# Convolution filter matrices on 112 partitions, first-stage stores on the scalar engine's queue, raw weights loaded in thirds

## Chip, cores and metric

The kernel runs on one core of a Trainium2 chip. The metric is the device time of the core in microseconds, median over runs; less is better. One execution was also recorded by the hardware profiler. Its engines are called PE (matrix multiply), PEld (weight load of PE), DVE (vector), ACT (scalar), POOL (GpSimd) and SP (which only issues transfers here).

## What is computed

The input `x` is 32 images of 384 channels of 28 by 28, all in float32. The reference is a ConvNeXt block followed by a gating layer:

```
y = depthwise_conv7x7(x, dw_w) + dw_b              # 384 channels, each with its own 7x7 filter
y = layernorm over channels(y) * ln_g + ln_b
y = gelu(y @ w1 + b1)                              # 384 -> 1536
y = grn(y) (per image, over the pixels) ; y = y @ w2 + b2        # 1536 -> 384
x = x + y
out = sigmoid(x + logits(mean, max, min of each channel of x))
```

## The kernel before

The work has a first stage (the depthwise convolution, with the preparation of the weights) and then, image by image, an up projection (`up`), a down projection (`down`) and the gate (`gate_store`). The two projections use schemes with fewer products than the plain matrix product: blocks of the weights are added and subtracted beforehand into combined weights (`form_w`, 15 for `w1`, 38 for `w2`), which the first stage stores to DRAM (`u1d`, `u2d`) and the later stages load again. Everything after the first stage keeps its instructions and nearly its order; the change is in the first stage and in the few operations that lead out of it.

**How the convolution is done on PE.** A row group of `RW`=4 image rows is one contraction. In the kernel before, each image row is padded from 28 to `PW`=32 columns, so a group is 128 elements on 128 partitions. For each channel a banded matrix of the 49 filter taps is needed. A sequence of `FL`=355 numbers for each channel lies in DRAM (`fs`), and row p of the matrix is that sequence read from p elements further on; `load_t` (L416) makes the matrices of `TC`=8 channels with one transfer, `tmat<-fs`, whose DRAM side steps by one element for each partition. A step `s` of the stage handles 8 channels for all 32 images; there are `NK`=48 steps and four buffers `tmat`. `load_t(s+3)` is issued at the start of step `s`.

**Input.** `load_x` (L449) loads tile `i`: 32 channels of 4 images, one (channel, image) pair on each of 128 partitions, 784 elements each. Eight tiles make a group of 32 channels, that is four steps. `pad_x` (L468) copies a tile to a padded buffer `xpad` (POOL for the first eight tiles, ACT for the other 88), `turn_x` (L477) transposes it in seven 128-column pieces on PE into PSUM (`pt`), and copies those with DVE and ACT to `xt`. `spread` spreads these over the steps of the group before.

**Convolution.** `conv` (L653) does a pair of channels: six matmuls into one PSUM tile `pc` of four; DVE transposes the pair in 32 by 32 blocks into `yt` (L682) and adds it to `acc` (L690), ACT squares it into `sq` (L696), POOL adds the squares to `ssum` (L702). After four pairs `yt` is stored to `yd` in DRAM (L837). Two buffers hold `yt`.

**Weights.** `w1` and later `w2` are loaded raw into `ws` (table `later`, issued at L789); each of these is preceded by a one-column copy on POOL that makes the load wait (L788). `center_w` folds the layer norm into `w1`. From step `U1`=11 on, `form_w` (L543) makes the combined `w1` blocks, from `U2`=23 on those of `w2`, on POOL (L550, L556) and ACT (L553), three buffers `u` in turn; the store of a block is issued at the end of the step after (L853).

**Order.** The Tile framework records the instructions of each engine and may move those that are not marked; `keep` marks an instruction to stay in program order. Within an engine, and within the list of transfers that an engine issues, order is fixed: in the kernel before SP issues all the loads and the stores `yd<-yt`, `u1d<-u`, `u2d<-u`. The lines that decide what follows a wait are

```
load_t(s + 3)
...
nc.sync.dma_start(yd[:, s * TC : (s + 1) * TC, :], yt)
...
for dst, u in stores:
    nc.sync.dma_start(dst, u)
```

**Way out of the stage.** The last two steps are done in halves of 16 images; `first_image` prepares image 0, `finish` (L710) turns `acc` and `ssum` into the factor of the layer norm and stores it (`rsd`), and `normed` (L307) applies it to image 1 with the reloaded `rb`.

Of the kernel before, what the change touches and what calls it, by code (L numbers as in the profile page):

```python
# [8 lines left out]
F32 = mybir.dt.float32  # L9
AF = mybir.ActivationFunctionType  # L10
ALU = mybir.AluOpType
AX = mybir.AxisListType

P = 128
C = 384
CB = C // P
FF = 4 * C
# [12 lines left out]
RW = 4  # L30
NJ = HW // RW
PW = P // RW
XC = 32
TC = 8
YC = 16
# [162 lines left out]
def convnext_gate_kernel(  # L198
# [109 lines left out]
    def normed(b, cbs=range(CB)):  # L308

        if b not in accs:  # L310
            accs[b] = (
                xp.tile([P, CB, NT], F32, tag="x", name=f"acc_{b}") if b == 1 else room_acc
            )
        for cb in cbs:
            nc.vector.scalar_tensor_tensor(  # L315
                accs[b][:, cb].rearrange("p (r w) -> p r w", w=HW), rows(yis[b][:, cb]),
                dwb_t[:, cb : cb + 1], rows(rbs[b]), ALU.add, ALU.mult,
            )

    def affine(eng, out, in_, mul, add):  # L320
        if eng is nc.vector:
# [38 lines left out]
    with ExitStack() as one:  # L360
        tp = one.enter_context(tc.tile_pool(name="tp", bufs=1))
        xtp = one.enter_context(tc.tile_pool(name="xtp", bufs=2))
        ufp = one.enter_context(tc.tile_pool(name="ufp", bufs=3))
        ycp = one.enter_context(tc.tile_pool(name="ycp", bufs=2))
        psx = one.enter_context(tc.tile_pool(name="psx", bufs=3, space=bass.MemoryType.PSUM))
        psb = one.enter_context(tc.tile_pool(name="psb", bufs=1, space=bass.MemoryType.PSUM))
        psc = one.enter_context(tc.tile_pool(name="psc", bufs=4, space=bass.MemoryType.PSUM))
        sqp = one.enter_context(tc.tile_pool(name="sqp", bufs=2))
        finp = one.enter_context(tc.tile_pool(name="finp", bufs=1))

        scr = yip.tile([P, CB, NQD, YR], F32, tag="yi", name="scr")
# [27 lines left out]


        NT2 = 4
        tmat = [tp.tile([P, TC, FL], F32, name=f"tmat_{i}") for i in range(NT2)]
        nc.vector.memset(tab, 0.0)

        def sequences(cb):
# [12 lines left out]
        def load_t(s, parts=1):  # L418
            base = fs[s * TC // P]
            n = TC // parts  # L420
            for i in range(parts):
                nc.sync.dma_start(
                    tmat[s % NT2][:, i * n : (i + 1) * n, :].rearrange("p c m -> p (c m)"),
                    bass.AP(
                        tensor=base.tensor,
                        offset=base.offset + (s * TC % P + i * n) * FL,
                        ap=[[1, P], [1, n * FL]],
                    ),
                )


        NPAD = 3
        xpad = [tp.tile([P, HW, PW], F32, name=f"xpad_{i}") for i in range(NPAD)]
        for t in xpad:
            nc.gpsimd.memset(t[:, :, HW:], 0.0)
        NX = C // XC
        NG = B // NB
        NXI = 8
# [26 lines left out]

        keep = tc.keep_in_program_order

        def pad_x(i):  # L468
            dst = xpad[i % NPAD][:, :, :HW]
            src = xis.pop(i).rearrange("p (r w) -> p r w", w=HW)  # L470
            if i < NG:
                nc.gpsimd.tensor_copy(dst, src)
            else:
                keep(nc.scalar.activation(dst, src, AF.Identity))

        def turn_x(i, h, xt, eng=nc.vector):

            g = i % NG
            xv = xt.rearrange("p c (j b) -> p j c b", j=NJ)
            j0, j1 = 4 * h, min(NJ, 4 * h + 4)  # L480
            pt = psx.tile([P, 4, P], F32, tag="pt", name=f"pt_{i}_{h}")
            for j in range(j0, j1):
                keep(
                    nc.tensor.transpose(  # L484
                        pt[:, j - j0, :],
                        xpad[i % NPAD][:, j * RW : (j + 1) * RW, :].rearrange("p r w -> p (r w)"),
                        ident,
                    )
                )
            dst = xv[:, j0:j1, :, g * NB : (g + 1) * NB]  # L490
            src = pt[:, : j1 - j0, :].rearrange("p j (c q) -> p j c q", q=NB)
            if eng is nc.vector:
                keep(eng.tensor_copy(dst, src))
            else:
                keep(eng.activation(dst, src, AF.Identity))  # L495

        def new_xt(k):
            return xtp.tile([P, XC, N], F32, tag="xt", name=f"xt_{k}")


        w1r = ws.rearrange("p (k f) -> p k f", f=FF)
        w1v = ws.rearrange("p (k t m c) -> p t k m c", t=KT, m=3, c=P)
        w2v = ws.rearrange("p (t k m c) -> p t k m c", t=KD, k=4, c=P)
        U1, U2 = 11, 23
        stores = []
        SG = 20

# [93 lines left out]

        AHEAD = NG

        def pad_next(i):
            if i < GT:
                pad_x(i)
                if i + AHEAD < GT:
                    load_x(i + AHEAD)

        for i in range(AHEAD):  # L610
            load_x(i)
        xt = new_xt(0)
        for i in range(NG):
            pad_x(i)
            if i == 0:
                load_t(0, 2)
                nc.sync.dma_start(dwb, cvec[0:1, :].broadcast_to([P, C]))
            if i == NG - 2:
                for cb in range(CB):
                    if cb:  # L620
                        keep(sequences(cb))
                    keep(nc.scalar.dma_start(fs[cb][P:, :], zrow))
            if i == NG - 2:

                nc.gpsimd.tensor_copy(tmat[1][:, 0, :1], xpad[i % NPAD][:, 0, :1])
                load_t(1)
            if i + AHEAD < GT:
                load_x(i + AHEAD)
            for h in range(2):
                turn_x(i, h, xt, (nc.vector, nc.scalar)[h])  # L630
        pad_next(NG)

        later = {
            2: (
                ws.rearrange("p (cb f) -> p cb f", f=FF),
                w1.rearrange("(cb p) f -> p cb f", p=P),
            ),
            U2 - 3: (
                ws.rearrange("p (fb c) -> p fb c", c=C),
                w2.rearrange("(fb p) c -> p fb c", p=P),  # L640
            ),
            1: (cv, cvec.rearrange("v (cb p) -> p v cb", p=P)),
            4: (fv, fvec.rearrange("v (fb p) -> p v fb", p=P)),
            6: (awt[:, 0], aw[0].rearrange("(cb p) r -> p cb r", p=P)),
            7: (awt[:, 1], aw[1].rearrange("(cb p) r -> p cb r", p=P)),
            8: (w22b, w22.broadcast_to([P, R])),
# [64 lines left out]
        def finish(half, b0, b1):  # L711

            def part(v):
                return v.rearrange("p (j b) -> p j b", b=B)[:, :, b0:b1]

            rs, s2 = (part(fin[:, i]) for i in range(2))
            mu, va = (part(acc[:, i]) for i in range(2))
            keep(nc.vector.tensor_tensor(mu, mu, va, ALU.add))
            keep(
                nc.vector.tensor_reduce(  # L720
                    s2,
                    ssum.rearrange("p c (j b) -> p j b c", b=B)[:, :, b0:b1],
                    AX.X, ALU.add,
                )
            )
            keep(nc.vector.tensor_scalar(mu, mu, dws, 1.0 / C, ALU.add, ALU.mult))
            keep(nc.vector.tensor_tensor(va, mu, mu, ALU.mult))
            keep(nc.vector.scalar_tensor_tensor(va, s2, 1.0 / C, va, ALU.mult, ALU.subtract))
            keep(nc.vector.tensor_scalar(va, va, 0.0, EPS, ALU.max, ALU.add))
            nc.scalar.activation(s2, va, AF.Sqrt)  # L730
            keep(nc.vector.reciprocal(rs, s2))
            keep(nc.vector.transpose(fin[:, 2], fin[:, 0]))
            nc.sync.dma_start(rsd[half], fin[:, 2])

        STEPS_K = SK * PAIRS
# [4 lines left out]
        def spread(k, q, xn):  # L740
            for n in plan[q]:
                g, h = divmod(n, 2)
                i = k * NG + g
                if h == 0:
                    pad_next(i + 1)
                turn_x(i, h, xn, (nc.vector, nc.scalar)[h])

        def first_image(part):

# [25 lines left out]
        for s in range(NK):  # L775
            k, si = divmod(s, SK)
            if s + 3 < NK:
                if s == 0:
                    for i in range(2, 4):
                        nc.gpsimd.tensor_copy(tmat[i][:, 0, :1], xpad[i % NPAD][:, 0, :1])  # L780
                        if i == 2:
                            load_t(i)
                load_t(s + 3)
# [44 lines left out]
            elif s < NK - 2:  # L828
                for c2 in range(PAIRS):
                    conv(s, c2, yt, xt, 0, B)  # L830
                    q = (s - U1 + 4) * PAIRS + c2
                    if 0 <= q < 4 * PAIRS:
                        for n in range(q * 3 // 2, (q + 1) * 3 // 2):
                            center_w(n)
                    if k + 1 < NX:
                        spread(k + 1, si * PAIRS + c2, xn)
                nc.sync.dma_start(yd[:, s * TC : (s + 1) * TC, :], yt)  # L837
                yt = new_yt(f"yt_{s + 1}")
                if s == 35:
                    yi = yis[0] = yip.tile([P, CB, NQD, YR], F32, tag="yi", name="yi_0")  # L840
# [9 lines left out]
                gate_weights()  # L850
                nc.vector.tensor_reduce(dws, dwb, AX.X, ALU.add)
            for dst, u in stores:
                nc.sync.dma_start(dst, u)  # L853
            stores.clear()
            for i in range(NS):
                if s != U1 + i * 3 // 5:
# [62 lines left out]
    def up(b, hooks):  # L919
# [6 lines left out]
        for t2 in range(0, KT, 2):  # L926
            for i, (opnd, _, bk, first, acts) in enumerate(UPSTEPS):
                for t in (t2, t2 + 1):
# [16 lines left out]
                    for src, how, to in acts:  # L945
                        p, d = banks[t, src][:, :NH], z[to]
                        if how == "copy":
                            ins = nc.scalar.activation(d, p, AF.Identity)  # L948
                            if b < 2:
                                tc.keep_in_program_order(ins)  # L950
                        elif how == "add":
                            nc.vector.tensor_tensor(d, d, p, ALU.add)  # L952
# [335 lines left out]
```

## Time and profile before

| | |
|---|---|
| time, median of 3 runs (lowest to highest) | 3091.12 us (3090.16 to 3092.08) |
| profiled execution: its own time, its span | 3089.71 us, 3087.7 us |
| PE busy | 3011.4 us (98%) |
| ACT, DVE, POOL busy | 1808.4, 1994.1, 2438.7 us |
| moved by DMA in the first 540 us | 173.12 MB, 321 GB/s |
| first convolution matmul, last convolution matmul | 20.2 us, 540.7 us |

The page has a row of digits for each engine over the span in 40 equal slices of 77 us (9 is 90% or more). In answers by stretch of time a row gives begin and end, length, then busy time and number of instructions for PE, PEld, DVE, ACT and POOL, the granted PE clock as a share of full speed, the busy share of the 16 DMA engines, and GB/s. In lists of waits a row gives who waited, for whom, the total in us, how often, and the longest. In lists of transfers a row gives the number, the size of each, and the median from issue to landing.

### The profile page before, as it was taken

What the parts mean: (1) busy time and instruction counts of PE and PEld (TensorE: products, weight loads), DVE (VectorE), ACT (ScalarE), POOL (GpSimd) and SP (SyncE); (2) the same over time, 40 slices, a digit from 0 to 9 for tenths busy, and PEclk for the clock granted to TensorE, in tenths of its full rate; (3) what the DMA queues carried; (4) which work ended last, traced back from release to release, by engine and by line L of the source; (5) the groups of instructions that cost most, each with busy time, mean ns of one, the idle gap of its engine ahead of it and who ended that gap; (6) DMA issues with size and microseconds to landing.
All of it is one profiled execution on the core that took longest, in us unless ns stands there. A gap on an engine that the chain in (4) does not pass through costs nothing.

```text
span 3087.7 us, 44113 instructions
## 1 busy us (share of the span) xinstructions
PE 3011.4 (98%) x14435; PEld 2434.4 (79%) x14435; DVE 1994.1 (65%) x4554; ACT 1808.4 (59%) x3004; POOL 2438.7 (79%) x1829
## 2 busy tenths in 40 slices
PE   7999989889999999999999999999999999999998
PEld 7999989467777777777777777777777777777777
DVE  4565546766666666666666666666666666666666
ACT  3454555556666666666666666666666666666661
POOL 3365857389888888888888888888888888888897
PEclk9999999999999999999999999999999999999999
DMA  9799988555666666666666666666666666666546
GB/s 367 263 333 356 335 324 264 174 165 188 202 199 196 200 198 200 198 197 200 199 199 200 199 200 202 200 203 200 202 201 202 199 200 201 201 201 202 194 153 201
DMA packets 288476, 673.24 MB, mean 218 GB/s; under 512 B 31199, under 2 KB 111610, under 8 KB 282234
## 3 DMA queue, kind: packets, MB, share of 16 engines
q1 hardware_dynamic: 275156, 631.62, 62.2%
q10 hardware_dynamic: 13094, 38.80, 3.3%
q8 instruction: 118, 1.93, 0.3%
q14 instruction: 108, 0.88, 0.1%
HBM read 575.57 MB, written 94.76 MB: 217 GB/s over the span
## 4 chain that ended last, share of the span: by engine, by line
PE 86%; DVE 5%; POOL 4%; DMA 2%; ACT 1%; issue 1%; SPq 0%; DVEq 0%; ACTq 0%; POOLq 0%
PE ph_C L941 14%; PE ph_A L941 12%; PE ph_B L941 11%; PE pz_A L1071 8%; PE pz_C L1071 8%; PE pz_F L1071 7%; PE pz_D L1071 7%; PE pc L675 4%; PE pc L679 3%; PE pc L677 3%; PE pz_H L1071 2%; PE pz_I L1071 2%; PE pz_E L1071 2%; PE pt L484 2%; DVE room L315 2%
## 5 line engine op out<-in xcount | busy, mean ns | idle before, releaser
L324 ACT ACTIVATE y<-y,fv,gsc 128x784 f32<-128x784 f32 x372 | 359.1, 1031 | 464.8 <-DVE gsc L979 464.8
L1032 POOL TENSOR_TENSOR d_room<-y 128x588 f32<-128x588 f32 x253 | 364.4, 1442 | 289.6 <-PE pz_B L1071 192.2
L941 PE MATMUL ph_C<-room,ws 128*128 128x392 f32 x1240 | 464.6, 497 | 9.1 <-DVE y L952 3.8
L900 ACT ACTIVATE y<-y,b1f 128x784 f32<-128x784 f32 x384 | 349.9, 944 | 200.9 <-DVE y L958 179.0
L941 PE MATMUL ph_B<-room,ws 128*128 128x392 f32 x1240 | 459.6, 493 | 6.8 <-ACT y L948 4.3
L941 PE MATMUL ph_A<-room,ws 128*128 128x392 f32 x1240 | 458.8, 492 | 2.0 <-POOL room L356 2.0
L1032 POOL TENSOR_TENSOR d_room<-d_room,y 128x588 f32<-128x588 f32 x308 | 440.7, 1435 | 16.8
L941 PEld LDWEIGHTS ph_C<-room,ws 128*128 128x128 f32 x1240 | 234.0, 191 | 193.8 <-DVE y L956 28.5
L941 PEld LDWEIGHTS ph_A<-room,ws 128*128 128x128 f32 x1240 | 235.8, 190 | 175.6 <-POOL room L356 2.7
L941 PEld LDWEIGHTS ph_B<-room,ws 128*128 128x128 f32 x1240 | 234.7, 190 | 171.2 <-ACT y L948 5.0
L702 POOL TENSOR_TENSOR ssum<-ssum,sq 128x896 f32<-128x896 f32 (+1 forms) x100 | 201.5, 2015 | 184.2 <-ACT sq L696 183.8
L913 ACT ACTIVATE junk<-y 128x784 f32<-128x784 f32 x384 | 329.0, 857 | 9.0
L1032 POOL TENSOR_TENSOR d_room<-y,d_room 128x588 f32<-128x588 f32 x214 | 306.0, 1436 | 26.9 <-PE pz_D L1071 15.8
L356 POOL TENSOR_TENSOR room<-room 128x392 f32<-128x392 f32 x303 | 303.4, 1018 | 11.9
L696 ACT ACTIVATE sq<-pc,dwb 128x224 f32<-128x224 f32 x368 | 144.5, 444 | 227.0 <-DVE acc L690 211.4
L1032 POOL TENSOR_TENSOR y<-y 128x588 f32<-128x588 f32 x180 | 258.6, 1437 | 7.1
L682 DVE STREAM_TRANSPOSE yt<-pc 128x448 f32<-128x448 f32 x184 | 119.5, 649 | 208.3 <-PE pc L679 194.9
L954 DVE TENSOR_TENSOR y<-y,ph_B 128x392 f32<-128x392 f32 x256 | 137.2, 556 | 155.2 <-ACT y L900 123.5
L952 DVE TENSOR_TENSOR y<-y,ph_C 128x392 f32<-128x392 f32 x384 | 212.4, 561 | 25.2
L675 PE MATMUL pc<-xt,tmat 128*128 128x224 f32 x736 | 203.2, 358 | 2.6 <-ACT xt L495 2.6
L1071 PE MATMUL pz_A<-d_room,u 128*128 128x196 f32 x1050 | 202.9, 329 | 0.1
L1071 PEld LDWEIGHTS pz_A<-d_room,u 128*128 128x128 f32 x1050 | 178.8, 190 | 7.7 <-POOL d_room L1032 0.4
(265 smaller groups left out, 6374.6 us busy)
## 6 DMA issues: line engine op xcount, KB each, us to landing
u<-u2d SPq DMA_DIRECT2D x487, 384.0 KB, 3.8
ws<-u1d SPq DMA_DIRECT2D x384, 320.0 KB, 3.0
tmat<-fs SPq DMA_DIRECT2D x47, 1420.0 KB, 8.8
ws<-u2d SPq DMA_DIRECT2D x121, 384.0 KB, 3.8
yi<-yd SPq DMA_DIRECT2D x95, 448.0 KB, 6.3
yd<-yt SPq DMA_DIRECT2D x46, 896.0 KB, 6.3
x<-in_x SPq DMA_DIRECT2D x32, 1176.0 KB, 5.5
out<-x ACTq DMA_DIRECT2D x31, 1176.0 KB, 9.2
```

Source lines behind the costliest of these rows:

```text
L324: eng.activation(out, in_, AF.Identity, bias=add, scale=mul)
L356: tc.keep_in_program_order(eng.tensor_tensor(d, o[in0], o[in1], op))
L675: keep(nc.tensor.matmul(po, t[:, c, P : 2 * P], xc, start=True, stop=False))
L696: nc.scalar.activation(part(sq)[:, cy % SQ + ci], part(pc[:, :, :N])[:, ci], AF.Square, bias=dwb[:, cc + ci : cc + ci + 1], scale=1.0,)
L702: nc.gpsimd.tensor_tensor(part(ssum), part(ssum), part(sq), ALU.add)
L900: ins = nc.scalar.activation(y, y, AF.Gelu, bias=b1f[:, f : f + 1], scale=1.0)
L913: ins = nc.scalar.activation(junk, ys[b][:, f, :], AF.Square, accum_out=ssqs[b][:, f : f + 1])
L941: nc.tensor.matmul(banks[t, bk][:, :NH], wts[t][:, i % UG, :], o[opnd], start=(first == 1), stop=True, skip_group_check=True,)
L952: nc.vector.tensor_tensor(d, d, p, ALU.add)
L954: nc.vector.tensor_tensor(d, d, p, ALU.subtract)
L1032: nc.gpsimd.tensor_tensor(d[0], o[a][0], o[c][0], ALU.add if sign == "+" else ALU.subtract)
L1071: nc.tensor.matmul(pz[:, :NQ4], wt[:, i % UD, t, :], o[opnd][0][:, t, :], start=(first and t == 0), stop=(t == KD - 1), skip_group_check=True,
```

## The change

The padded copy is gone, with `xpad` and its memsets: row groups are 4 times 28 = 112 elements (`KP`), a group is transposed as it was loaded, and the filter matrices and `xt` lie on 112 partitions. The DRAM side of `tmat<-fs` now counts 4 by 28 rows, so as to leave out the four padding rows in each 32. The stores of the first stage move from SP's queue to ACT's and are kept in program order. `w1` and `w2` are loaded in three parts each, at steps 3, 4, 5 and 21, 22, 23; `U1`, `U2` become 12 and 24; `ufp` has four buffers in place of three, `sqp` three in place of two. The next `x` tile of a slot is loaded after the transposes of the tile in it, not after its padding. The matrices of `center_w`'s second part come four at a time. `normed` of image 1 stays in program order, the nine DVE operations of `finish` lose their `keep` and may be moved, and so may the copies of image 0 in its first two blocks of `up`.

```
+KP = RW * HW
@@ normed
-            nc.vector.scalar_tensor_tensor(
+            ins = nc.vector.scalar_tensor_tensor(
...
+            if b == 1:
+                tc.keep_in_program_order(ins)
@@ pools
-        ufp = one.enter_context(tc.tile_pool(name="ufp", bufs=3))
+        ufp = one.enter_context(tc.tile_pool(name="ufp", bufs=4))
-        sqp = one.enter_context(tc.tile_pool(name="sqp", bufs=2))
+        sqp = one.enter_context(tc.tile_pool(name="sqp", bufs=3))
-        tmat = [tp.tile([P, TC, FL], F32, name=f"tmat_{i}") for i in range(NT2)]
+        tmat = [tp.tile([KP, TC, FL], F32, name=f"tmat_{i}") for i in range(NT2)]
@@ load_t
                         offset=base.offset + (s * TC % P + i * n) * FL,
-                        ap=[[1, P], [1, n * FL]],
+                        ap=[[PW, RW], [1, HW], [1, n * FL]],
@@ pad_x
-        def pad_x(i):
-            dst = xpad[i % NPAD][:, :, :HW]
-            src = xis.pop(i).rearrange("p (r w) -> p r w", w=HW)
-            if i < NG:
-                nc.gpsimd.tensor_copy(dst, src)
-            else:
-                keep(nc.scalar.activation(dst, src, AF.Identity))
@@ turn_x
-            pt = psx.tile([P, 4, P], F32, tag="pt", name=f"pt_{i}_{h}")
+            pt = psx.tile([P, 4, P], F32, tag="pt", name=f"pt_{i}_{h}")[:KP]
...
-                        pt[:, j - j0, :],
-                        xpad[i % NPAD][:, j * RW : (j + 1) * RW, :].rearrange("p r w -> p (r w)"),
-                        ident,
+                        pt[:, j - j0, :], xis[i][:, j * KP : (j + 1) * KP], ident
@@
-            return xtp.tile([P, XC, N], F32, tag="xt", name=f"xt_{k}")
+            return xtp.tile([KP, XC, N], F32, tag="xt", name=f"xt_{k}")
-        U1, U2 = 11, 23
+        U1, U2 = 12, 24
-        def pad_next(i):
-            if i < GT:
-                pad_x(i)
-                if i + AHEAD < GT:
-                    load_x(i + AHEAD)
+        def load_next(i):
+            del xis[i]
+            if i + AHEAD < GT:
+                load_x(i + AHEAD)
+        def hold(dst, i):
+            nc.gpsimd.tensor_copy(dst, xis[i][: dst.shape[0], :1])
@@ later
-            2: (
-                ws.rearrange("p (cb f) -> p cb f", f=FF),
-                w1.rearrange("(cb p) f -> p cb f", p=P),
-            ),
...
+                3 + cb: (
+                    ws.rearrange("p (cb f) -> p cb f", f=FF)[:, cb],
+                    w1[cb * P : (cb + 1) * P, :],
+                )
+                for cb in range(CB)
...
+                U2 - 3 + i: (
+                    ws.rearrange("p (fb c) -> p fb c", c=C)[:, 4 * i : 4 * i + 4],
+                    w2[4 * i * P : (4 * i + 4) * P, :].rearrange("(fb p) c -> p fb c", p=P),
+                )
+                for i in range(3)
@@ finish
-            keep(nc.vector.tensor_tensor(mu, mu, va, ALU.add))
+            (nc.vector.tensor_tensor(mu, mu, va, ALU.add))
...
@@ spread
-                if h == 0:
-                    pad_next(i + 1)
                 turn_x(i, h, xn, (nc.vector, nc.scalar)[h])
+                if h:
+                    load_next(i)
@@ center_w
-                    q = (s - U1 + 4) * PAIRS + c2
-                    if 0 <= q < 4 * PAIRS:
+                    q = (s - U1 + 5) * PAIRS + c2
+                    if 0 <= q < 2 * PAIRS:
                         for n in range(q * 3 // 2, (q + 1) * 3 // 2):
                             center_w(n)
+                    elif q in (2 * PAIRS + 2, 2 * PAIRS + 5, 2 * PAIRS + 8):
+                        n = FB + 4 * ((q - 2 * PAIRS) // 3)
+                        for i in range(4):
+                            center_w(n + i)
@@ stores
-                nc.sync.dma_start(yd[:, s * TC : (s + 1) * TC, :], yt)
+                keep(nc.scalar.dma_start(yd[:, s * TC : (s + 1) * TC, :], yt))
...
             for dst, u in stores:
-                nc.sync.dma_start(dst, u)
+                keep(nc.scalar.dma_start(dst, u))
@@ up
-                            if b < 2:
+                            if b == 1 or (b == 0 and t2):
```

More of the change, by code (lines that the diff above doesn't have):

```diff
@@ L426, in load_t @@
                         offset=base.offset + (s * TC % P + i * n) * FL,
-                        ap=[[1, P], [1, n * FL]],
+                        ap=[[PW, RW], [1, HW], [1, n * FL]],
                     ),
                 )
[L432 to L435, printed above, removed]
         NX = C // XC
@@ L466, in convnext_gate_kernel @@
         keep = tc.keep_in_program_order
-        def pad_x(i):
-            dst = xpad[i % NPAD][:, :, :HW]
-            src = xis.pop(i).rearrange("p (r w) -> p r w", w=HW)
-            if i < NG:
-                nc.gpsimd.tensor_copy(dst, src)
-            else:
-                keep(nc.scalar.activation(dst, src, AF.Identity))
+        keep = tc.keep_in_program_order
         def turn_x(i, h, xt, eng=nc.vector):
@@ L613, in convnext_gate_kernel @@
         for i in range(NG):
-            pad_x(i)
             if i == 0:
@@ L623, in convnext_gate_kernel @@
             if i == NG - 2:
-                nc.gpsimd.tensor_copy(tmat[1][:, 0, :1], xpad[i % NPAD][:, 0, :1])
+                hold(tmat[1][:, 0, :1], i)
                 load_t(1)
-            if i + AHEAD < GT:
-                load_x(i + AHEAD)
             for h in range(2):
                 turn_x(i, h, xt, (nc.vector, nc.scalar)[h])
-        pad_next(NG)
+            load_next(i)
         later = {
-            2: (
-                ws.rearrange("p (cb f) -> p cb f", f=FF),
-                w1.rearrange("(cb p) f -> p cb f", p=P),
-            ),
[L638 to L641, printed above, removed]
+            **{
+                3 + cb: (
[3 more added lines that the diff above has]
+                for cb in range(CB)
+            },
+            **{
+                U2 - 3 + i: (
[3 more added lines that the diff above has]
+                for i in range(3)
+            },
             1: (cv, cvec.rearrange("v (cb p) -> p v cb", p=P)),
-            4: (fv, fvec.rearrange("v (fb p) -> p v fb", p=P)),
+            2: (fv, fvec.rearrange("v (fb p) -> p v fb", p=P)),
             6: (awt[:, 0], aw[0].rearrange("(cb p) r -> p cb r", p=P)),
@@ L717, in finish @@
             mu, va = (part(acc[:, i]) for i in range(2))
-            keep(nc.vector.tensor_tensor(mu, mu, va, ALU.add))
-            keep(
+            (nc.vector.tensor_tensor(mu, mu, va, ALU.add))
+            (
                 nc.vector.tensor_reduce(
@@ L725, in finish @@
             )
[L726 to L729, printed above, removed]
+            (nc.vector.tensor_scalar(mu, mu, dws, 1.0 / C, ALU.add, ALU.mult))
+            (nc.vector.tensor_tensor(va, mu, mu, ALU.mult))
+            (nc.vector.scalar_tensor_tensor(va, s2, 1.0 / C, va, ALU.mult, ALU.subtract))
+            (nc.vector.tensor_scalar(va, va, 0.0, EPS, ALU.max, ALU.add))
             nc.scalar.activation(s2, va, AF.Sqrt)
-            keep(nc.vector.reciprocal(rs, s2))
-            keep(nc.vector.transpose(fin[:, 2], fin[:, 0]))
+            (nc.vector.reciprocal(rs, s2))
+            (nc.vector.transpose(fin[:, 2], fin[:, 0]))
             nc.sync.dma_start(rsd[half], fin[:, 2])
@@ L743, in spread @@
                 i = k * NG + g
-                if h == 0:
-                    pad_next(i + 1)
                 turn_x(i, h, xn, (nc.vector, nc.scalar)[h])
+                if h:
+                    load_next(i)
         def first_image(part):
@@ L779, in convnext_gate_kernel @@
                     for i in range(2, 4):
-                        nc.gpsimd.tensor_copy(tmat[i][:, 0, :1], xpad[i % NPAD][:, 0, :1])
+                        hold(tmat[i][:, 0, :1], NG)
                         if i == 2:
```

## The prediction

> **What bounds the kernel now.** I read the page's slices first, then the first stage in stretches, then PE's waits there, then the transfers.
>
> ```profile
> PE   7999989889999999999999999999999999999998
> ...
> DMA  9799988555666666666666666666666666666546
> ```
>
> PE is busy nearly everywhere. The first seven slices (to 540 us) differ from the rest in the last row: there the DMA engines too are nearly full. The change works there.
>
> ```profile
> 20.00:120.00 100.00, 93.18 (x586) 89.11 (x587) 51.28 (x89) 46.19 (x104) 34.65 (x23) 0.97 0.96 350
> 120.00:160.00 40.00, 36.20 (x232) 34.97 (x232) 23.75 (x44) 16.22 (x36) 14.35 (x10) 0.96 0.61 213
> 160.00:240.00 80.00, 79.76 (x503) 76.36 (x502) 47.37 (x82) 46.06 (x102) 50.25 (x32) 1.00 0.98 341
> 240.00:520.00 280.00, 263.89 (x1615) 252.37 (x1614) 152.20 (x265) 147.01 (x332) 185.52 (x130) 0.97 0.91 327
> ```
>
> Undisturbed (160 to 240 us) PE is full, and a step takes about 10.2 us. Two resources bound the stage together: PE, and right behind it the DMA engines, 0.91 to 0.98 busy. PE's pauses are short:
>
> ```profile
> PE pt L484 <- ACT xpad L474: 22.0, 5, 8.8
> PE pt L484 <- POOL xpad L472: 6.8, 2, 6.2
> PE ph_C L941 <- DVE y L952: 4.9, 3, 3.8
> PE ph_B L941 <- ACT y L948: 4.3, 1, 4.3
> PE pm L588 <- DVE ws L597: 3.8, 2, 3.1
> ```
>
> From 20.2 to 540.7 us they sum to 26.7. After a long pause matmuls take twice their time for a while: from 60 to 80 us 72 matmuls (11.2 us at the undisturbed pace) and a pause of 6.3 leave 2.5 us lost; over the five long pauses about 10. Behind the pauses: at 64 us a store `yd<-yt` landed after 16 us behind the whole `w1`; at 300 and 415 us ACT sat for a `u` buffer (7.3, 9.2 us); at 248 us DVE waited for POOL's copy at L788.
>
> ```profile
> q1 hardware_dynamic: 53640, 171.41, 88.8%
> ...
> tmat<-fs SPq DMA_DIRECT2D x47, 1420.0 KB, 8.8
> yd<-yt SPq DMA_DIRECT2D x46, 896.0 KB, 6.3
> room<-in_x SPq DMA_DIRECT2D x84, 392.0 KB, 6.6
> ```
>
> The filter matrices are 68 MB of the stage's 171: the largest transfer by far, spread over 16 engines.
>
> [...] loads with 128, 112 or 16 rows outermost show 16 completion events each; `scr<-in_wfcT` (24 rows, 130.4 us) shows 13[...]; the one-row stores `fs<-scr` show 2. `room<-in_x` counts 32 by 4 in DRAM and 128 in SBUF, and shows 16. No transfer of before has fewer than 12 engines and many bytes. [...] the trace has the halving (two matmuls of L675 that otherwise take 0.38 us take 0.75 from 72 to 77 us).
>
> **The change part by part.**
>
> (1) *The filter load.* Its SBUF side has 112 rows outermost, its DRAM side 4 (times 28, step 32 and 1). [...] So each of the 47 loads (and the first in two halves) runs on four engines, 28 rows on each, in place of 8 rows on each of 16. Bytes fall by 12.5%, bytes per loaded engine rise 3.5 times. Price, from the trace's packet records: a row of 11360 bytes is one packet, median 426 ns (26.7 GB/s; mean 489 over the stage, 435 from 120 to 160 us, where the engines are less full). The work of one of the four engines over the stage, by medians:
> filter rows 48 x 28 x 0.426 = 572.5 us; `x` tiles 96 x 8 x 0.124 = 95.2; `yd` 46 x 8 x 0.272 = 100.1; `u1d` 15 x 32 x 0.027 = 13.0; `u2d` 38 x 8 x 0.065 = 19.8; `w1`, `w2` 12; constants, `fs` and the first `u1d` reloads 11. Sum 823 us.
> By the means of 120 to 160 us it is 882, by those of the whole stage 940. Below the medians: packets overlap a little (the busy share goes to 1.03 from 60 to 80 us), up to 6%, 775. I take 840: near the medians, since with four engines full and twelve mostly idle the total is under 200 GB/s, and the long packets of before come when 350 are moved.
> That is 17 us per step against PE's 10.2, or 12.7 with the half clock after each pause: PE waits for every filter load, with `load_t(s+3)` always issued ahead, so the four engines never run dry. First load at 1.3 us; some 6 us of the 840 follow the last filter load; from its landing PE has two steps in halves less what can start before, 14 us (18.9 for all of it, of which step 46's first half, 4.7, needs only the load before). Last convolution matmul: 1.3 + 840 - 6 + 14 = 849, before 540.7: **+309**. Lookahead of four buffers hides latency, not a missing rate.
>
> (2) *Padding gone.* ACT loses 88 copies of 0.858 us (75.5), POOL 8 of 0.84. Both lie beside PE's wait for the filter: nothing. Without that cover it takes ACT out of the chain DVE, ACT, pad, transpose, where 22.0 + 6.8 us were lost.
>
> (3) *Stores on ACT's queue.* 46 + 53 transfers, 0.3 to 0.9 us each to issue by the rows of L815, so 30 to 90 us on ACT, less than (2) frees at its middle. A store of `u` now makes ACT wait for POOL's last addition; behind it stand the squares, the copies to `xt`, so PE's `pc` and `pt`. SP waited thus:
>
> ```profile
> SPq L853 <- POOL u L556: 32.8, 9, 6.9
> ```
>
> Four `pc` tiles at about 2.4 us a pair cover some 7 us. Nothing here, as PE waits longer for the filter. SP keeps only loads and no longer stops for stores.
>
> (4) *Thirds, buffers, center_w.* `w1`, `w2` move the same bytes; a fourth `u` buffer puts a step (10 us, more than the 9.1 that such a store takes at most) between a store and the reuse; the fours of `pm` leave three pairs between them. Bounds: 0 to -12 us if PE were the bound; 0 now, covered by the filter. Two more copies at L788 may hold DVE 2.8 us each, covered alike. Startup likewise: padding and a vector reduction fewer ahead of the first matmul, 1 to 2 us, but the first filter load takes 28 x 2 x 0.22 = 12 us on four engines in place of 3.5.
>
> (5) *Way out.* PE lost 2.49 + 4.33 + 3.80 us at 543 to 563 us, the last two because DVE ran all of `finish` ahead of image 0's first results and then stood 5.2 us for `rb` in `normed`. With these rearranged PE could gain 10; but ten POOL additions for image 1 follow `normed`, and the stretching and GELU of image 0 queue behind them; `rb` cannot land earlier. **-4** (0 to -9). The other stages keep their order: 0.
>
> Sum: +309 - 4 = +305 on the profiled execution's 3089.7, which is 1.4 below the median: 3395 + 1.4, so 3396.
>
> **The rivals.**
>
> *A. The load runs on 14 or 16 engines after all* [...]. Decided by one number: a loaded engine needs 112/k x 0.426 + 5.2 us a step, which is under 10.2 for k of 10 and up. At 16 it is 8.2, less than before, and PE is the bound again: 26.7 of pauses and 10 of half clock go, 2 at the start, 4 on the way out, some 4 us of new pauses come. 3091 - 39 = 3052, between 3040 and 3070. For it: `x` is loaded with a 32 by 4 side on 16 engines. Against: 32 is a multiple of 16, so this says nothing of 4; and the 24-row load took just 12.
>
> *B. Four engines, but at the stage's mean price or worse*, since both queues meet on the same four: 940 us, 3495.
>
> *C. ACT's queue becomes the bound.* If POOL were late with `u` by over 7 us beyond its step on average, each of the 30 steps with such stores would cost PE the rest: at 9 us late 60 us, 3112 with A's gains set against it. POOL's additions per step are at most 8 us with 4.2 of squares, against 10.2: late by 2 once or twice. It needs A first.
>
> **Numbers.** Some 0.2% (6 us) is what a measurement of this kernel can tell from no change. Main case with B as its upper end 0.92, A 0.06, C and a draw 0.02. The range takes the packets' overlap (775: 3330) and stops at 930 (3485). Faster 0.06, same 0.01, slower 0.93.
>
> **What would show it.** PE's main wait would be the convolution on the DMA `tmat<-fs`, near 300 us over some 45 pauses; that load's issue to landing goes from 8.8 to over 40 us; `tmat<-fs` shows 5 completion events; in the longer first stage the DMA share drops to 0.5 to 0.6 though PE waits for DMA; PE's share there is about 0.6 and its clock below 0.9. If `tmat<-fs` lands in under 10 us, and the last convolution matmul comes near 500 us, part 1 is wrong and A is right. A stage between 640 and 780 us would mean a cheaper packet than I took.

## The result and the profile after

The changed kernel takes 3452.4 us (median of 4 runs, 3448.1 to 3458.9) against 3090.6 us: a ratio of 1.117, with an interval of 1.115 to 1.119. The profiled execution took 3448.96 us, its span is 3446.9 us: 359.3 us more than the profiled execution before.

All of it lies in the first stage. The last convolution matmul ends at 903.4 us instead of 540.7 (+362.7). What follows takes 2543.4 us instead of 2547.0 (-3.6).

The slices (77 us a digit until now, 86 in this longer span), with the clock row between:

```profile
PE   6586665666799999999999999999999999999998
...
PEclk8778787778899999999999999999999999999999
DMA  5645555554645665655666666655666666655546
```

In the first ten slices PE is at 5 to 8 tenths, its clock at 7 or 8, and the DMA row, which was 7 to 9 there, is at 4 to 6. No row is full, so what limits the stage is not a row of its own here.

The same stretch as a window (length, then busy time and count of PE, PEld, DVE, ACT, POOL, then clock, DMA share, GB/s):

```profile
20.00:903.00 883.00, 572.38 (x3113) 535.32 (x3114) 285.03 (x514) 192.16 (x511) 299.33 (x209) 0.79 0.52 181
```

The mean share is 0.52 of 16 engines: 8.3 engines' worth. This is a mean over engines of which four are full. The filter rows (5264 packets of 11360 bytes) add up to 2432.8 us in the first 884 us, 608 on each of four engines. What remains from 10 us on comes to 302 us an engine if spread evenly over 16. The sum is 910 us, for 874 us of elapsed time between 10 and 884 us: a little overlap, and no room for a pause. `tmat<-fs` shows 5 completion events in each of its 49 loads, one 1.1 us after the issue and the other four after 28.3 to 34.0 us (medians). Of its rows more than four are in flight in 1% of the time that any is (before: more than 16 in 4%), and from 20 to 880 us fewer than four packets of all transfers together are in flight in 1.5% of the time. So a filter load runs on four engines, and by this and the sum above these hardly ever stand idle.

That four engines are full and twelve are not shows in the other transfers as well. An `x` tile has 16 completion events, read here as those of 16 shares, one for each engine. Twelve of them come within 4.9 us of the issue, the other four after 15.9 to 20.2 us (medians of 84 tiles, worked out from the trace's events); before, all 16 come within 6.5 us. `scr<-in_wfcT` (24 packets) has 13 events in both kernels, the first 0.5 us after the issue; the other twelve come from 7.5 to 8.5 us before, and now eight by 2.8 us and four from 12.4 to 15.3.

PE's waits in the stage (us, times, longest):

```profile
PE pc L671 <- ACT sq L692: 128.1, 14, 16.6
PE pt L477 <- ACT xt L486: 70.7, 8, 22.1
PE pc L671 <- ACT xt L486: 40.1, 5, 15.6
PE pc L671 <- DMA tmat<-fs: 29.7, 6, 10.2
PE pt L477 <- DVE xt L484: 28.5, 7, 8.5
PE pb L564 <- DMA ws<-in_w: 16.7, 1, 16.7
```

They sum to 314 us in 41 pauses. Only 30 us carry the name of the filter load; most carry ACT's. That looks like a slow ACT, but ACT itself is busy 192 of 883 us. The chain that ended last, in order of time (start, length, what), says what stood behind it:

```profile
470.85 32.15 DMA tmat<-fs
504.05 36.47 DMA tmat<-fs
...
558.86 18.84 DMA xi_last<-in_x
577.76 34.83 DMA tmat<-fs
613.93 34.80 DMA tmat<-fs
...
799.44 35.85 DMA tmat<-fs
835.73 15.82 DMA u2d<-u
...
853.07 31.45 DMA tmat<-fs
```

One transfer follows the other, and of the pieces of compute and issue between them (left out) each is short. A landing is counted at the last completion event, and four of the 16 come late, so `x` tiles and stores wait for the four full engines too. From issue to the last completion event, medians worked out from the trace's events: `tmat<-fs` 34.0 us (8.8 before), `room<-in_x` 20.2 (6.5), `u1d<-u` 28.3 (6.0), `yd<-yt` 11.2 (6.3). How ACT comes to stand for them can be read from the events too. In the traces of before and after, all transfers of SP and ACT count their completion on the same eight semaphores (101 to 108), and in the first stage each one is issued only after the one before it on its semaphore has landed (275 times of 275 before, 279 of 279 after). For this ACT stood 360 us of the stage at its stores, in 35 waits, mostly until a filter load (165) or an `x` tile (140) of SP had landed; in e1_k16 below it is 33 us. The list of ACT's waits has part of it, at an operation that reads neither `tmat` nor `room`:

```profile
ACT u L544 <- DMA tmat<-fs: 90.8, 4, 28.5
ACT u L544 <- DMA room<-in_x: 79.2, 5, 24.7
```

Behind the stores stand ACT's squares, which free PE's `pc`. So ACT passes on the lateness of the four engines. It is one path of it and not its cause: e3_before_k4 and e8_stores_sp below, where ACT stood 8 us and not at all for this, are as slow.

### The profile page after: what moved, and what is told of

It reads as the page before. It is cut to its first block, busy times and chain, and to the rows that moved or that the text cites. A ratio compares the mean times of both kernels' runs of the same rounds, so it can differ in the third digit from the quotient of the medians.

```text
span 3446.9 us, 43986 instructions
## 1 busy us (share of the span) xinstructions
PE 3090.9 (90%) x14435; PEld 2498.4 (72%) x14435; DVE 1990.0 (58%) x4554; ACT 1736.7 (50%) x2916; POOL 2432.2 (71%) x1822
## 4 chain that ended last, share of the span: by engine, by line
PE 68%; DMA 22%; POOL 4%; DVE 3%; issue 1%; ACT 1%; SPq 0%; ACTq 0%; DVEq 0%; POOLq 0%
PE ph_C L941 12%; DMA tmat<-fs 11%; PE ph_A L941 10%; PE ph_B L941 10%; PE pz_A L1071 7%; PE pz_C L1071 7%; PE pz_F L1071 6%; PE pz_D L1071 6%; DMA room<-in_x 4%; PE pz_H L1071 2%; DMA u1d<-u 2%; PE pz_I L1071 2%; PE pz_E L1071 2%; POOL d_room L1032 1%; DVE room L316 1%; DMA ws<-in_w 1%
## 5 line engine op out<-in xcount | busy, mean ns | idle before, releaser
L671 PE MATMUL pc<-xt,tmat 112*128 112x224 f32 x736 | 236.4, 407 | 198.0 <-ACT sq L692 128.1
L359 POOL TENSOR_TENSOR room<-room 128x392 f32<-128x392 f32 x303 | 303.5, 1018 | 11.9
L671 PEld LDWEIGHTS pc<-xt,tmat 112*128 112x128 f32 x736 | 143.0, 222 | 204.5 <-ACT sq L692 131.8
L673 PE MATMUL pc<-xt,tmat 112*96 112x192 f32 x736 | 205.2, 365 | 0.0
```

The source lines that it names most:

```text
L359: tc.keep_in_program_order(eng.tensor_tensor(d, o[in0], o[in1], op))
L671: keep(nc.tensor.matmul(po, t[:, c, P : 2 * P], xc, start=True, stop=False))
L673: nc.tensor.matmul(lo, t[:, c, 2 * P : T0 + MW], after, start=False, stop=False)
```

## Experiments

Filter rows are the packets of 11360 bytes; their length stands as mean / median. "Step" is the mean distance between landings of successive filter loads. The engines are read from the completion events of a filter load: 4 from 5 events (after, e3_before_k4), 8 from 9 (e2_k8), 16 from 16 (before, e1_k16); e5, e6, e9, e11 and e12 have the load of before, e8 has that of after. For e4, e7 and e10 the number is the author's estimate from the rows of the access pattern.

| kernel | engines x rows each | us | ratio, interval | filter row, ns | step, us | last conv. matmul ends, us |
|---|---|---|---|---|---|---|
| before | 16 x 8 | 3090.6 | 1 | 489 / 426 | 10.3 | 540.7 |
| after | 4 x 28 | 3452.4 | 1.117 (1.115 to 1.119) | 462 / 426 | 18.0 | 903.4 |
| e1_k16 | 16 x 7 | 3090.3 | 1.000 (0.998 to 1.002) | 635 / 636 | 10.3 | 540.2 |
| e10_k14 | 14 x 8 | 3117.2 | 1.008 (1.006 to 1.009) | 661 / 673 | 11.1 | 573.5 |
| e2_k8 | 8 x 14 | 3203.8 | 1.036 (1.033 to 1.039) | 509 / 429 | 12.6 | 643.2 |
| e3_before_k4 | 4 x 32 | 3592.8 | 1.163 (1.157 to 1.168) | 497 / 427 | 20.8 | 1052 |
| e4_four | 14 x 2, four loads | 3221.6 | 1.042 (1.040 to 1.043) | 753 / 806 | 13.0 | 673.4 |
| e7_four_k7 | 7 x 4, four loads | 3275.2 | 1.060 (1.058 to 1.061) | 520 / 426 | 14.5 | 733.1 |
| e5_rows128 | 16 x 8 | 3077.1 | 0.993 (0.990 to 0.996) | 533 / 426 | 9.9 | 536.1 |
| e11_rows128_sp | 16 x 8 | 3046.8 | 0.985 (0.984 to 0.987) | 477 / 426 | 9.6 | 502.8 |
| e8_stores_sp | 4 x 28 | 3445.0 | 1.115 (1.112 to 1.117) | 457 / 427 | 17.6 | 899.3 |
| e6_rest128 | 16 x 8 | 3135.3 | 1.014 (1.013 to 1.016) | 538 / 427 | 11.3 | 589.5 |
| e9_rest128_sp | 16 x 8 | 3080.7 | 0.996 (0.995 to 0.998) | 480 / 426 | 10.2 | 532.9 |
| e12_pad2_u4 | 16 x 8 | 3064.0 | 0.991 (0.989 to 0.993) | 478 / 426 | 9.8 | 516.8 |

e4, e6, e8, e9 and e12 compute the whole reference. The others (e1, e2, e3, e5, e7, e10, e11) load other rows of the same table for most partitions, so they leave out the right filters and serve for timing alone.

**The number of engines (e1_k16, e2_k8, e3_before_k4).** One line of `load_t` in each:

```diff
-    ap=[[PW, RW], [1, HW], [1, n * FL]],     # after: 4 by 28 rows
+    ap=[[1, KP], [1, n * FL]],               # e1_k16: 112 rows
+    ap=[[15, 8], [1, 14], [1, n * FL]],      # e2_k8: 8 by 14 rows
-    ap=[[1, P], [1, n * FL]],                # before: 128 rows
+    ap=[[31, 4], [1, 32], [1, n * FL]],      # e3_before_k4: 4 by 32 rows
```

> The changed kernel, with one edit: the DRAM side of the filter load counts 112 rows in one dimension (step 1) in place of 4 by 28 (steps 32 and 1). Bytes, packets and everything else stay; 84 of the 112 partitions get other rows of the same table than the filter's. Theory (the outermost 4 puts the load on four engines, and these are full for the whole first stage): 16 completion events, 7 rows on each of 16 engines, 7 x 0.426 + 5.2 = 8.2 us of engine work a step, below PE's 10.2; PE bounds the stage, its last convolution matmul comes near 505 us, the whole near 3052 us (3040 to 3070). Rival 1 (the stores on ScalarE's queue are what holds PE, as PE's waits in the trace go through the squares and copies of ScalarE): the queue is as before, so about 3450. Rival 2 (112 partitions and the unpadded transposes cost by themselves): about 3450.

> The changed kernel, with the DRAM side of the filter load as 8 by 14 rows (steps 15 and 1)[...]. Again other rows of the same table. Theory: 9 completion events, 14 rows on each of 8 engines, 14 x 0.426 + 5.2 = 11.2 us a step by the medians, 11.8 by the means that the changed kernel shows (0.462 for a filter row): 50 steps put the last convolution matmul between 560 and 600 us, 3105 to 3150 us in all, with the DMA share about 0.8. It is the dose between 4 and 16. Rivals 1 and 2: about 3450.

> The kernel before, with one edit: the DRAM side of its filter load, 128 rows with step 1, becomes 4 by 32 rows (steps 31 and 1), so that it can't be read as one dimension; 96 partitions get other rows of the table. Stores, padding, pools and order stay as before. Theory: 5 completion events, 32 rows on each of four engines; 32 x 0.426 + 5.2 = 18.8 us a step by the medians, 20.5 by the means of the changed kernel: last convolution matmul between 910 and 1010 us, 3460 to 3560 us in all. Rivals 1 and 2: nothing of theirs is in this kernel, so about 3091.

The completion events are 16, 9 and 5, with 112, 8 and 4 rows outermost in DRAM. With 16 engines the whole loss is gone, with ScalarE's queue and the 112 partitions as in the changed kernel; with four engines the kernel before, which has neither, is 502 us slower. Both rivals fall: the split is the cause, and alone enough.

But each number missed its range to the slow side. e1_k16 gave 3090 and not 3052. Its window of the stage shows one reason:

```profile
20.00:520.00 500.00, 476.07 (x2924) 458.51 (x2924) 274.23 (x480) 189.97 (x487) 285.43 (x198) 0.95 0.95 309
```

The DMA share is 0.95, although 12.5% fewer filter bytes move than before (0.91, 325 GB/s): a row now takes 635 ns, so 16 engines are as full as PE. The long rows are not all of the 38 us: e5_rows128, with shares of 8 rows, brings 13 of them, and the stores back on SP (e11_rows128_sp, 3046.8) bring the rest.

**What makes a row long (e4_four, e5_rows128, e7_four_k7, e10_k14).** Theory P of the expectations below is an assumption, and its figures are the author's estimates: how the rows of a load are divided among the engines sets how long a row takes. Why it should, no trace shows. Of the 28 rows of one of e4_four's loads, 2 fall to each of 14 engines, and a row takes 753 ns on average; for 4 on each of 7 engines the theory gives 430 to 480. That can be tried:

```diff
-    ap=[[PW, RW], [1, HW], [1, n * FL]],
+    ap=[[1, HW], [1, n * FL]],               # e4_four: four loads, offset r * PW, to t[28 * r : 28 * r + 28]
+    ap=[[5, HW // 4], [1, 4], [1, n * FL]],  # e7_four_k7: the same four loads as 7 by 4 rows
+    ap=[[1, P], [1, n * FL]],                # e5_rows128: 128 rows to 128 partitions, 112 used
+    ap=[[9, 14], [1, 8], [1, n * FL]],       # e10_k14: 14 by 8 rows
```

> The changed kernel, with each filter load written as four loads of 28 rows, one for each group of 28 partitions; it computes the whole reference. Theory: 28 rows go to 14 engines, 2 rows on each for each load, 8 a step: 8 x 0.426 + 5.2 = 8.6 us a step, below PE's 10.2. Near 3052 us as with 16 engines (3040 to 3075); 141 more issues on SP at 0.4 to 0.9 us each have room there. Rivals 1 and 2: about 3450. It is also the version that could beat both kernels.

> The four loads of 28 rows each, with their DRAM side as 7 by 4 rows (steps 5 and 1; other rows of the table), so that each runs on 7 engines with 4 rows each in place of 14 engines with 2 rows. Theory P: [...] packets 430 to 480 ns, 16 x 0.45 + 5.2 = 12.4 us a step, 3180 to 3240 us: half the engines in the same time. Rival (a packet's length is set by the DRAM side or by the issue on SP[...]): packets stay near 750 ns, 16 x 0.75 + 5.2 = 17.2 us a step, 3430 to 3470 us.

> The changed kernel, with the filter load fetching 128 rows with step 1 into 128 partitions (the load of the kernel before), of which the convolution uses the first 112; other rows of the table than the filter's on 84 of them. Against the 112 plain rows it moves 14% more filter bytes and changes nothing else: transposes without padding, stores on ScalarE's queue and all the rest stay. Theory P ([...]packets lengthen from 489 to 635 ns on average): packets back to 430 to 500 ns, PE bounds the stage again, 3050 to 3075 us. Rival Q (the second loaded queue lengthens the packets): they stay near 635 ns, 8 x 0.635 + 5.2 = 10.3 us a step and more bytes, 3090 to 3130 us.

> The changed kernel, with the DRAM side of the filter load as 14 by 8 rows (steps 9 and 1; other rows of the table): 14 engines with 8 rows each. Theory P [...]: packets of 600 ns and more, 8 x 0.62 + 5.2 = 10.2 us a step and above, 3090 to 3150 us. Rival (the number of engines alone counts, packets as with 128 rows, 533 ns): 8 x 0.533 + 5.2 = 9.5 us a step, 3055 to 3085 us.

e4_four missed its range by 147 us: its 14 engines take 806 ns a row at the median. With half the engines (e7_four_k7) the median is 426. The windows of e4_four and then e7_four_k7:

```profile
20.00:630.00 610.00, 510.35 (x2906) 481.33 (x2906) 272.46 (x475) 189.91 (x479) 283.78 (x196) 0.90 0.87 249
```

```profile
20.00:700.00 680.00, 521.82 (x2883) 490.38 (x2882) 270.66 (x470) 190.41 (x477) 281.96 (x195) 0.86 0.67 223
```

Twice the engines move 12% more, at a share of 0.87 against 0.67: the share counts the longer rows (753 against 520 ns on average) as work. The median was near what theory P gave, the mean (520 ns) and the time not quite: 3275 instead of 3240 at most. By difference (14.5 less 16 x 0.520) the other transfers cost 6.2 us a step and not 5.2. In both, SP stood some 455 us at its issues until the transfer before on the same semaphore had landed, as there are four times as many filter loads; what that adds to their times was not separated. e5_rows128 separates the rest: the same 16 engines, the same queues, plain rows in DRAM and 14% more filter bytes than e1_k16, and the row falls from 635 to 533 ns on average (500 was the upper end of what was expected), to 426 at the median. More rows come in less time, and more bytes in all (332 against 309 GB/s), which neither a second queue nor the DRAM side nor the total rate explains. The second queue has a smaller effect of its own, which rival Q had: with the stores back on SP the same loads' rows take 477 ns in place of 533 (e11 against e5) and 480 in place of 538 (e9 against e6). e10_k14 (661) fits theory P: 8 rows on each of 14 engines take longer than 8 on each of 16. So in the loads tried here a row's length goes with the way that they are divided among the engines. What it is in 16 by 7, 14 by 8 or 14 by 2 that makes rows long was not shown: no packet in the traces carries its engine or its partitions.

**The queue of the stores (e6_rest128, e8_stores_sp, e9_rest128_sp, e11_rows128_sp, e12_pad2_u4).** e8, e9 and e11 put two lines back:

```diff
-    keep(nc.scalar.dma_start(yd[:, s * TC : (s + 1) * TC, :], yt))
+    nc.sync.dma_start(yd[:, s * TC : (s + 1) * TC, :], yt)
-    keep(nc.scalar.dma_start(dst, u))
+    nc.sync.dma_start(dst, u)
```

e6_rest128 is the kernel before with all parts of the change but the 112 partitions; e9_rest128_sp is that with the stores on SP; e11_rows128_sp is e5_rows128 with the stores on SP.

> The changed kernel with the stores of yt and u back on SP's queue, the filter load on four engines as it is. Theory (the four engines are full from the first to the last filter load, and PE's waits that pass through ScalarE only pass the lateness on): filter loads land 18 us apart as before, 3430 to 3470 us. Rival 1 (the store that waits on ScalarE, with the squares and copies behind it, is what holds PE): 150 us or more come back, under 3300.

> The kernel before with the change's other parts and without the 112 partitions: stores of the first stage on ScalarE's queue, w1 and w2 in thirds, the shifted starts of the two weight stages, the rearranged constants and centering, finish and normed reordered. Padding and the load of 128 rows stay, and with them the memory of the two added buffers, so 3 u and 2 sq buffers as before. It computes the whole reference. By the prediction's steps (3) to (5): 4 us less on the way out and 0 to 12 in the stage, 3075 to 3090 us. Rival (ScalarE, which still pads, can't also carry the stores: a store that waits for POOL holds the paddings behind it, and PE's transposes): 3095 to 3130 us.

> The version with padding, 128 rows and the change's other parts, with the stores of yt and u back on SP's queue as in the kernel before; it computes the whole reference. The one with stores on ScalarE's queue took 3135 us. Theory (ScalarE's queue: a store of u waits there for POOL, and the padding copies behind it, which PE's transposes need, come late; 41.5 us of PE's waits are on them): without the stores on ScalarE 3075 to 3092 us, PE's wait for xpad back near 20 us. Rival (the later weight stages, the thirds or the rearranged constants cost it): stays above 3115 us.

> The unpadded version with the load of 128 rows (3077 us with stores on ScalarE's queue; other rows of the table on 84 partitions), with the stores of yt and u back on SP's queue. It prices the store move where the filter load hides nothing. The prediction's step (3) put it at nothing: 3070 to 3085 us. Rival 1 (the move is a gain, since SP's loads no longer stand behind stores that wait for POOL): 3090 to 3110 us here. Rival 2 (the move costs): under 3065 us here.

On four engines the queue makes no clear difference: 3445.0, and the intervals meet. The same lateness only takes another path, now through DVE, which can't have its `yt` back (first list; PE's waits in the second):

```profile
DVE yt L678 <- DMA yd<-yt: 493.7, 45, 17.8
```

```profile
PE pt L477 <- DVE xt L484: 120.1, 21, 9.6
PE pc L671 <- ACT xt L486: 108.9, 11, 15.7
```

So the rival "ScalarE's queue holds PE" falls for the changed kernel. Where the filter load is not slow, it holds: 54.6 us between e6 and e9 and 30.4 between e5 and e11 (of which some 20 may be the clock, last section), both in favour of SP. In e6_rest128, PE and then ACT (timeline; start, length, engine, line, what, idle before it and releaser):

```profile
469.04 1.75 PE L486 MATMUL pt<-ident,xpad 128*128 128x128 f32 x7 [5.48 <-ACT xpad L476]
```

```profile
455.52 0.90 ACTq L865 DMA_DIRECT2D u2d<-u  x1
...
457.08 0.52 ACT L555 ACTIVATE u<-ws 128x384 f32<-128x384 f32 x1 [0.47 <-ACT xpad L476]
465.98 0.52 ACT L555 ACTIVATE u<-ws 128x384 f32<-128x384 f32 x1 [8.38 <-DMA u2d<-u]
...
468.10 0.88 ACT L476 ACTIVATE xpad<-room 128x784 f32<-128x784 f32 x1
```

ACT issues a store of `u` when its own order comes to it, soon after needs the buffer that this very store must free (its last completion event is at 465.90), and stands 8.4 us; the padding that PE needs is queued behind. A store of `u` to `u2d` also takes longer there, 8.1 us from issue to landing at the median against 4.6 in e9. Over the stage, ACT's wait for the store of `u` and PE's for the padding, first in e6 and then in e9:

```profile
ACT u L555 <- DMA u2d<-u: 65.2, 11, 8.4
...
PE pt L486 <- ACT xpad L476: 41.5, 12, 5.5
```

```profile
ACT u L555 <- DMA u2d<-u: 26.8, 5, 7.1
...
PE pt L486 <- ACT xpad L476: 19.0, 10, 4.9
```

e9 already beats both kernels, the one before by 10 us; which of its parts brings that was not tried. What it still loses is the same chain, so the last experiment takes the buffer for it from the padding:

```diff
-    ufp = ... tile_pool(name="ufp", bufs=3)      NPAD = 3
+    ufp = ... tile_pool(name="ufp", bufs=4)      NPAD = 2
```

> The 3081 us version (padding and 128 rows kept, stores on SP's queue, the change's other parts) with the memory of one of the three padding buffers given to a fourth u buffer; it computes the whole reference. Theory (ScalarE stands 33.8 us for a u buffer whose store has not landed, and the padding copies behind it are what PE waits 19 us for): with four buffers that wait goes, PE's wait for xpad falls under 10 us, 3060 to 3075 us. Rival (two padding buffers are too few, so that a copy waits for the transposes of the tile before): PE's wait for xpad rises, 3085 us and above.

```profile
PE pt L486 <- ACT xpad L476: 7.8, 4, 3.2
```

ACT's wait for `u` is gone from the list, PE's is 7.8 us, and the time is 3064.0 us: 27 us (0.9%) less than before, the fastest version here that leaves nothing out. e11_rows128_sp is at 3046.8 with other filter rows: what unpadded transposes would bring, if a load of the right rows for them ran at full rate. None of the loads tried here is one.

## Why the prediction was right, step by step

The forecast was 3396 us, range 3330 to 3485; measured 3452.4.

- **Step 1, four engines: right.** 5 completion events, and e1 and e3 show it as the cause. Until then it was the author's estimate: the trace of before has no transfer with many bytes and fewer than 13 completion events. The size was short by 54 us (+309 against +363), and the term is the work of a loaded engine, taken at 840 us "near the medians". Per step it was 28 x 0.426 = 11.9 of filter and 5.2 of the rest, 17.1; measured are 28 x 0.462 = 12.9 and about 6.1, less some 5% of overlap, 18.0. The ground for the medians, that under 200 GB/s packets stay short, failed: with only 181 GB/s moved, `x` rows take 177 ns on average (median 124). What counts is probably the load of the single engine and not the total; packets carry no engine number, so this is not shown. The sum by the means of 120 to 160 us, 882, was nearer: the last filter load landed at 884.5. The other 5 us are the tail: the last two steps took 19 us after it, not 14.
- **The form of the wait: wrong.** It was to be the convolution on `tmat<-fs`, near 300 us over some 45 pauses. The sum (314 us, 41 pauses) is right, the name is on 30 us only. The step took the four engines as a wall for the filter alone; every transfer with shares on them lands late, and its consumers carry the wait, as do the engines that issue the next transfer on its semaphore. The filter's landing came to 34 us, not over 40. PE share 0.65, clock 0.79 and DMA share 0.52 were as said.
- **Step 2, padding hidden:** nothing in the changed kernel contradicts it. The 6.8 us that it adds to the 22.0 of the chain lie before the first convolution matmul, so they are no part of it. That the padding chain costs when uncovered is seen in e9 (19.0 us) and e12 (7.8).
- **Step 3, stores on ScalarE's queue at nothing: right under the cover named** (e8: 7 us, intervals meeting), and its price without cover, which it left at some 7 us of slack, is larger: 55 us with padding, 10 to 30 without. It looked at POOL being late with `u`, for which ACT's stores in the changed kernel waited 3 us. What came with the filter load on four engines is the wait for a semaphore (360 us on ACT; SP, which was to stop no longer, stood 466 us), and without it the store's own lateness, through the `u` buffer (65.2 us in e6).
- **Step 4 at nothing, bounds 0 to -12: consistent.** In e9, without the two buffers, the end of the convolution moves by -7.8.
- **Step 5, way out -4: right**, -3.6 (2547.0 to 2543.4), and -3.3 in e9.
- **Rival A (14 or 16 engines, 3052):** the case did not come, but its price was wrong. It kept 0.426 us a row for any k, where e10 and e1 take 0.66 and 0.64, so the point of k = 10 from which PE would bound lies near 16; and it put the stores' queue at nothing. With shares of 8 rows and the stores on SP, e11 comes to 3046.8. **Rival C**: ScalarE's queue does hold PE in e6, but through the store's landing and not through a late POOL.

## What to carry to other kernels

Before re-laying data, write both access patterns of the load that it changes and look at the outermost counts: here a 4 there left four engines of 16 and a step of 18.0 us in place of 10.3, and four buffers of lookahead didn't help against a rate. In the profile this showed as a DMA share near a half (0.52) while everything waited for DMA, with the waits named after innocent engines; the chain in order of time and the completion events named the real one: few events on the slow load (5), and on the other transfers a few that come late (four of an `x` tile's 16, after 15.9 to 20.2 us). And put a store on the queue of an engine that computes only if the buffers behind it outlast the store's landing (8.1 us at the median for `u` in e6_rest128, where ACT waited 65.2 us in all), and if its issue needn't wait for other transfers (360 us of ACT in the changed kernel).

## What the runs showed of the hardware that was not expected

- Twice the engines were not twice the rate: 14 engines (e4_four) take 806 ns at the median for a row that takes 426 on seven (e7_four_k7), and 249 GB/s moved in place of 223. 16 engines with 7 rows each take 635 on average, with 8 rows each 533.
- In the profiled run of e5_rows128 PE had half its clock for 40 us, after a gap of 1.6 us at 498 and though it was never idle from 500 to 530:

```profile
480.00:500.00 20.00, 18.41 (x112) 17.73 (x111) 11.38 (x22) 10.06 (x24) 16.85 (x12) 0.99 0.78 289
500.00:540.00 40.00, 36.09 (x181) 35.84 (x180) 20.69 (x44) 10.41 (x34) 14.55 (x13) 0.50 0.48 107
```

  That is some 20 us of its 30 against e11, which has 1.00 in the whole stage. It does not come in every execution: four of e5's six took 3076 to 3079 us at a mean clock of 0.986 to 0.988, the other two 3053 and 3059 at 0.995 and 0.994. The same pause of 1.6 us is followed by full clock in e1 and e10. What brings it about was not found.
